# A selective-scan block with a planned order of issue: longer planned TensorE times, and state columns copied after the C product

## The chip, the cores and the metric

The kernel runs on one core of one Trainium2 chip. The metric is the device time of one execution in microseconds (us); the time before is the median of three runs, 4419.52 us (4413.35 to 4423.57). A further execution was taken with the hardware profiler; all rows of the profile come from that one.

Engines are named as in the profile: PE is TensorE (matmuls; PEld is its weight load), DVE is VectorE, ACT is ScalarE, POOL is GpSimd, SP is SyncE, which issues all transfers here.

## The reference

One layer: a normalised Mamba block with a residual, then a normalised linear layer whose weights are dequantised, with a residual. 4096 positions, model width 1024, inner width 2048, 16 states per channel. Cut to what matters:

```python
proj = layernorm(x) @ in_proj_w                    # 1024 -> 2 * 2048
x, z = split(proj); xc = silu(causal_conv4(x))
ssm_p = einsum('bdl,ed->ble', xc, x_proj_w)         # 64 + 16 + 16 rows
dt_r, Bm, Cm = rmsnorm of its three parts
dt = softplus(einsum('blr,dr->bdl', dt_r, dt_proj_w) + dt_bias)
def step(h, inp):                                   # over the positions
    h = exp(dt_t[..., None] * A) * h + dt_t[..., None] * B_t[:, None, :] * x_t[..., None]
    y = einsum('bdn,bn->bd', h, C_t)
    return (h, y)
y = (ys + D_param * xc) * silu(z)
x = hidden + einsum('bdl,hd->blh', y, out_proj_w)
x = x + layernorm(x) @ dequantised(W).T + bias
```

## The kernel before, in words

Channels lie on the 128 partitions, positions along the free axis. Positions are taken in chunks of 512 (`TC`) for the matmuls and in blocks of 256 (`TS`) for the scan. The scan is cut into units: a chunk, a block `s`, a group `g` of four channel tiles, a half `hf` of it (two channel tiles), and a pair `k` of states. That makes 1024 units, each with a scan of two channel tiles, two states and 256 positions. A unit has three steps:

- `unit_b`: POOL multiplies `u` (dt times x) by B into `h`, a tile of 128x1024 (L972), and ACT puts the carried first columns into it (L974, four columns). Three units ahead.
- `unit_e`: ACT makes four exponentials, 128x256 each, into two PSUM tiles `da` (L984), one for each state. One unit ahead.
- `unit_s`: DVE scans, one `tensor_tensor_scan` of 128x512 for each state (L997). Then ACT copies the last column of each scan to `state` (L1001), from which the next block's first columns are made, and the scan is multiplied by C. PE then transposes the product 128x128 at a time and adds it up in `py` (L1014, eight matmuls a unit); at the end of a half, ACT copies `py` out, and an epilogue transposes it back and multiplies by `silu(z)`.

`unit_s` has two forms. With `on_pool` the scan writes to `h`, and POOL multiplies all of `h` by C in one instruction (L1005). Otherwise the scan writes over `da` in PSUM, and DVE multiplies it into `h`, one instruction of 128x512 for each state (L1003). Which form a unit takes is decided while the program is recorded, by comparing the summed planned times of POOL and of DVE (`order.load`).

Buffers: seven `h` tiles (`hp`), four `da` tiles in four PSUM banks (`ps_a`), one `py` (`ps_y`). Accesses to a PSUM bank by different engines are kept in order, readers too; that is how a copy out of `da` and a product out of `da` come to wait for each other in the order in which they are recorded.

Around the units run the large matmuls as background: input projection (`ips`, `zps`), output projection (`ops`) and the last layer (`fps`). Each is three passes on split fp32 values, 128x512 wide (L610, L611, L612). `pull` records as much of them between units as keeps pace with the units.

The order in which every engine issues its instructions is not the recorded one. The class `Order` records all instructions with their accesses (`read`), gives each a planned time (`cost`: the time until the engine can take the next, and the time until the result is there), and plays the whole program through (`schedule`). At each step the engine that can start earliest issues the ready instruction that was recorded first; buffers, transfers and the delay until another engine sees a result (`SEE`) are part of that play. `tie` then fixes the resulting order on every engine. On the chip each engine takes its instructions in that fixed order, and waits where one's inputs are late.

For PE, `cost` has three cases: matmuls into `xps`, wide float32r matmuls by their number of columns `n`, and the rest, which are fp32 transposes.

Of the kernel before, what the change touches and what calls it, by code (L numbers as in the profile page):

```python
# [20 lines left out]
ALU = mybir.AluOpType  # L21
# [6 lines left out]
TS = 256  # L28
# [19 lines left out]
class Order:  # L48
# [112 lines left out]
    def cost(self, r, e, n, silu):  # L161

        op = r.opcode
        if e == 0:
            name = str(r.outs[0])
            if "xps" in name:
                g = 223
            elif "float32r" in str(r.ins[0].dtype):
                g = 6 + 0.434 * n
            else:  # L170
                g = 0.85 * n
            return g, g + 164
        if e == 1:
            if op == "LoadActFuncSet":
                return 1300, 1300
            if op == "TensorCopy":
                d = 170 + 0.815 * n
            else:
                wide = sum(getattr(x, "bass_ap", None) is not None for x in r.ins) > 1
                d = 200 + 1.02 * n if wide else 195 + 0.84 * n  # L180
            if n < 32:
                return 95, 190
            if silu:
                d += 1400
            elif str(r.outs[0].bass_ap.space).endswith("PSUM"):
                return d - 56, d + 17
            return d - 100, d
        if e == 2:
            d = 180 + 2.15 * n
            if op == "TensorTensor" and "pow" in str(r.op):  # L190
                d = 400 + 157 * n
            return d - 40, d
        if e == 3:
            d = 140 + 1.05 * n
            if op == "BNStats":
                d = 676
            elif op == "TensorScalarPtr" and r.is_tensor_tensor_scan:
                d = 150 + 2.085 * n
            elif op == "TensorScalarPtr" and r.is_scalar_tensor_tensor:
                d = 230 + n  # L200
            return d - 82, d
        return 430, 0
# [126 lines left out]
def mamba_ffn_kernel(ctx, tc, hs, in_w, conv_w, conv_b, xp_w, dt_w, dt_b, a_log, d_par, out_w,  # L329
                     dt_ln, b_ln, c_ln, q_scales, q_vals, f_bias, out):  # L330
    nc = tc.nc
# [11 lines left out]
    sizes = [TC] * (L // TC)  # L343
# [4 lines left out]
    NCH = len(sizes)  # L348
# [637 lines left out]
    def unit_s(v, py):  # L986

        c, s, g, hf, k = v["at"]
        cc = bts[c, s, k][1]
        h, da = v.pop("h"), v.pop("da")  # L990
        cb_ = cc.unsqueeze(2).to_broadcast([P, 2, 2, TS])
        g0 = g * 4 + 2 * hf
        on_pool = order.load[2] + POOL_MORE < order.load[3]
        for n in range(2):
            flat = da[n].rearrange("p a b -> p (a b)")
            hflat = h[:, n].rearrange("p a b -> p (a b)")
            nc.vector.tensor_tensor_scan(hflat if on_pool else flat, flat, hflat, 0.0, ALU.mult, ALU.add)  # L997
        for n in range(2):
            last = (h[:, n] if on_pool else da[n])[:, :, TS - 1]
            if not (c == NCH - 1 and s == sizes[c] // TS - 1):  # L1000
                nc.scalar.copy(state[:, g0:g0 + 2, 2 * k + n], last)  # L1001
            if not on_pool:
                nc.vector.tensor_tensor(h[:, n], da[n], cb_[:, n], ALU.mult)  # L1003
        if on_pool:
            nc.gpsimd.tensor_tensor(h, h, cb_, ALU.mult)  # L1005
        hc = h
        terms = [(n, hc[:, n]) for n in range(2)]
        if k == 0:
            terms.insert(0, (-1, v["pre"][3][hf]))
        for n, src in terms:  # L1010
            for tb in range(NTS):
                for j in range(2):
                    i = tb * 2 + j
                    nc.tensor.matmul(py[:, i * P:(i + 1) * P], src[:, j, tb * P:(tb + 1) * P], ident, is_transpose=True,  # L1014
                                     start=(n < 0 and i == 0), stop=(k == N // 2 - 1 and n == 1), skip_group_check=True)
# [44 lines left out]
    state = cst.tile([P, ND, N], F32, name="state")  # L1060
# [104 lines left out]
    for i, v in enumerate(units):  # L1165
        c, s, g, hf, k = v["at"]
        if k == 0:
            py = ps_y.tile([P, TC], F32, tag="py", name="py")
        ahead(i + B_AHEAD, unit_b)
        ahead(i + E_AHEAD, unit_e)  # L1170
        unit_s(v, py)
        v.clear()
        if k == EPI_N and pend is not None:
            pull(until=("z", pend[0], pend[2], 2))
            with tc.high_priority(1000):
                epilogue(*pend)
            pend = None
        pull(total * min(1.0, (i + LEAD) / len(units)))
        b = blocks.index((c, s, g)) + 1
        if b < len(blocks):  # L1180
            if hf == 0 and k == PREP_N:
                if blocks[b][1:] == (0, 0):
                    pull(until=("x", c + 1))
                with tc.high_priority(1000):
                    pres[blocks[b]] = prep_group(*blocks[b])
            if g == NG - 1 and hf == 1:
                c2, s2, _ = blocks[b]
                bts[c2, s2, k] = load_bc(c2, s2, k)
        if k == N // 2 - 1:
            with tc.high_priority(1000):  # L1190
                yt = tmp.tile([P, NTS, 2, P], F32, tag="tmp", name="yt")
                nc.scalar.copy(yt.rearrange("p a b c -> p (a b c)"), py)
            pend = (c, s, g, hf, yt)
# [35 lines left out]
```

## Time and profile before

| What | Value |
|---|---|
| Median of three runs | 4419.52 us (4413.35 to 4423.57) |
| Profiled execution, its own time | 4422.55 us |
| Its span, first to last instruction | 4420.8 us |
| Mean granted TensorE clock | 0.968 |
| B product on POOL, L972, 1024 times | 2423.9 us, 2388 ns each |
| Exponentials on ACT, L984, 4096 times | 1858.6 us, 473 ns each |
| Scans on DVE, L997, 2048 times | 1378.4 us into `da`, 1044.9 us into `h` |
| C product on POOL, L1005, 441 times | 1055.4 us, 2396 ns each |
| Transposes into `py`, L1014, 8192 out of `h` | 1116.6 us, 280 ns each |

Busy time is the union of an engine's instructions, so a PE row's time can overlap its neighbours: PE's instructions are pipelined, and 280 ns for one does not mean one every 280 ns; the distance between starts tells that. A row of the waits says which engine's which line stood idle, and what ended the idle time. Idle time of an engine costs something only where that engine's next work is needed.

### The profile page before, as it was taken

To read this page: it belongs to the slowest core of one execution; us is meant where nothing else is said; L and a number is where in the kernel's file an instruction comes from. 1 tells how busy PE (TensorE), PEld (TensorE's weight loads), DVE (VectorE), ACT (ScalarE), POOL (GpSimd) and SP (SyncE) were. 2 spreads that over 40 slices of the span, in tenths; PEclk is the share of its full clock that TensorE was granted. 3 is DMA by queue.
4 is the path that set the end of the run, shared out by engine and by line. 5 is a ranking of instruction groups with operands and counts; after the bars stand their busy time and mean duration, and the time that the engine had idled before them with its cause. 6 is when DMAs were issued, how large, how long until landed. Compare 5 with 4: busy or idle time off the path is not lost.

```text
span 4420.8 us, 73712 instructions
## 1 busy us (share of the span) xinstructions
PE 4072.3 (92%) x23658; PEld 3451.4 (78%) x23658; DVE 3908.0 (88%) x4842; ACT 3573.4 (81%) x9854; POOL 3853.4 (87%) x2234
## 2 busy tenths in 40 slices
PE   8988899999988999999999999999999999998887
PEld 6767778777876887788777888788877878887776
DVE  5588889998999989999899999999989999998882
ACT  5788888888887888888888789888888877877671
POOL 0678799899997999999999999999998999999791
PEclk9989999999999999999999999999999999999987
DMA  8868866567678765987568875788566898988765
GB/s 261 270 226 286 289 215 217 178 201 222 187 249 273 238 216 174 298 263 246 180 209 272 254 255 184 250 277 277 189 200 215 302 320 264 308 256 275 241 223 189
DMA packets 693843, 1066.39 MB, mean 241 GB/s; under 512 B 63816, under 2 KB 488832, under 8 KB 692432
## 3 DMA queue, kind: packets, MB, share of 16 engines
q1 hardware_dynamic: 693456, 1061.68, 74.1%
q8 instruction: 187, 3.06, 0.3%
q14 instruction: 200, 1.64, 0.1%
HBM read 815.85 MB, written 245.63 MB: 240 GB/s over the span
## 4 chain that ended last, share of the span: by engine, by line
PE 47%; ACT 13%; POOL 13%; DVE 10%; DMA 8%; issue 4%; SPq 1%; DVEq 0%; POOLq 0%; ACTq 0%
PE py L1014 11%; POOL h L972 7%; ACT da L984 4%; DVE da L997 4%; POOL h L1005 4%; PE ops L610 3%; PE ops L611 3%; PE ops L612 3%; PE ips L610 3%; PE ips L612 3%; PE ips L611 3%; PE zps L610 2%; PE zps L611 2%; PE zps L612 2%; DVE h L1003 2%
## 5 line engine op out<-in xcount | busy, mean ns | idle before, releaser
L972 POOL TENSOR_TENSOR h<-xl,bb 128x1020 f32<-128x1020 f32 x1024 | 2423.9, 2388 | 214.7 <-PE py L1014 201.5
L984 ACT ACTIVATE da<-dt,amat 128x256 f32<-128x256 f32 x4096 | 1858.6, 473 | 186.0 <-DVE h L1003 143.4
L997 DVE TENSOR_TENSOR_SCAN da<-da,h 128x512 f32<-128x512 f32 x1166 | 1378.4, 1213 | 66.0 <-POOL h L972 26.5
L1014 PE MATMUL py<-ident,h 128*128 128x128 f32 x8192 | 1116.6, 280 | 97.9 <-POOL h L1005 73.7
L1014 PEld LDWEIGHTS py<-ident,h 128*128 128x128 f32 x8192 | 972.2, 144 | 219.2 <-POOL h L1005 103.1
L1005 POOL TENSOR_TENSOR h<-h,cc 128x1024 f32<-128x1024 f32 x441 | 1055.4, 2396 | 80.8 <-ACT state L1001 71.6
L997 DVE TENSOR_TENSOR_SCAN h<-da,h 128x512 f32<-128x512 f32 x882 | 1044.9, 1208 | 44.4 <-ACT da L984 32.5
L1003 DVE TENSOR_TENSOR h<-da,cc 128x512 f32<-128x512 f32 x1166 | 755.4, 677 | 49.0 <-ACT state L1001 48.0
L610 PE MATMUL ops<-yh,wt 128*128 128x512 f32 (+1 forms) x1152 | 457.2, 398 | 19.5 <-DMA yh<-y 5.8
L611 PE MATMUL ops<-yh,wt 128*128 128x512 f32 (+1 forms) x1152 | 431.4, 375 | 2.4 <-DMA yh<-y 2.2
L612 PE MATMUL ops<-yh,wt 128*128 128x512 f32 (+1 forms) x1152 | 431.0, 374 | 0.0
L610 PE MATMUL zps<-nh,wt 128*128 128x512 f32 x896 | 365.9, 408 | 6.9 <-DVE nh L409 2.8
L612 PE MATMUL zps<-nh,wt 128*128 128x512 f32 x896 | 358.4, 400 | 0.0
L611 PE MATMUL zps<-nh,wt 128*128 128x512 f32 x896 | 357.9, 399 | 0.0
L610 PE MATMUL ips<-nh,wt 128*128 128x512 f32 x768 | 316.1, 412 | 20.2 <-DVE ssm L721 8.4
L688 DVE SCALAR_TENSOR_TENSOR pre<-ips,cw,pre 128x511 f32<-128x511 f32 (+2 forms) x384 | 281.3, 733 | 48.6 <-ACT pre L685 41.6
L612 PE MATMUL ips<-nh,wt 128*128 128x512 f32 x768 | 307.2, 400 | 0.0
L611 PE MATMUL ips<-nh,wt 128*128 128x512 f32 x768 | 306.7, 399 | 0.0
L1001 ACT COPY state<-da 128x2 f32<-128x2 f32 x1098 | 158.8, 160 | 150.0 <-DVE da L997 144.5
L610 PEld LDWEIGHTS ops<-yh,wt 128*128 128x128 f32 x1152 | 223.0, 194 | 53.0 <-DVE xb L835 7.7
L612 PEld LDWEIGHTS ops<-yh,wt 128*128 128x128 f32 x1152 | 222.0, 193 | 36.4
L611 PEld LDWEIGHTS ops<-yh,wt 128*128 128x128 f32 x1152 | 223.6, 194 | 30.8 <-DMA yh<-y 4.7
(163 smaller groups left out, 7159.3 us busy)
## 6 DMA issues: line engine op xcount, KB each, us to landing
wt<-wi SPq DMA_DIRECT2D x416, 512.0 KB, 4.3
wt<-wo SPq DMA_DIRECT2D x288, 512.0 KB, 5.3
wt<-wf SPq DMA_DIRECT2D x144, 512.0 KB, 4.8
yh<-y SPq DMA_DIRECT2D x224, 256.0 KB, 6.2
xl<-xc SPq DMA_DIRECT2D x64, 512.0 KB, 6.3
bb<-b SPq DMA_DIRECT2D x128, 256.0 KB, 5.8
cc<-b SPq DMA_DIRECT2D x128, 256.0 KB, 6.4
ze<-sz SPq DMA_DIRECT2D x128, 256.0 KB, 4.2
```

Source lines behind the costliest of these rows:

```text
L610: nc.tensor.matmul(ps, wk[:, 0, k % 4, :], hi, start=(k == 0), stop=False)
L611: nc.tensor.matmul(ps, wk[:, 0, k % 4, :], lo, start=False, stop=False)
L612: nc.tensor.matmul(ps, wk[:, 1, k % 4, :], hi, start=False, stop=(k == KT - 1))
L688: nc.vector.scalar_tensor_tensor(o, ps[:, 0:sz - 3 + k], cw[:, m, k:k + 1], o, ALU.mult, ALU.add)
L972: nc.gpsimd.tensor_tensor(h[:, :, :, 1:], u[:, js, 1:].unsqueeze(1).to_broadcast([P, 2, 2, TS - 1]), bb[:, :, 1:].unsqueeze(2).to_broadcas ...
L984: nc.scalar.activation(da[n][:, j, :], dt[:, 2 * hf + j, :], AF.Exp, scale=amat[:, d, 2 * k + n:2 * k + n + 1])
L997: nc.vector.tensor_tensor_scan(hflat if on_pool else flat, flat, hflat, 0.0, ALU.mult, ALU.add)
L1001: nc.scalar.copy(state[:, g0:g0 + 2, 2 * k + n], last)
L1003: nc.vector.tensor_tensor(h[:, n], da[n], cb_[:, n], ALU.mult)
L1005: nc.gpsimd.tensor_tensor(h, h, cb_, ALU.mult)
L1014: nc.tensor.matmul(py[:, i * P:(i + 1) * P], src[:, j, tb * P:(tb + 1) * P], ident, is_transpose=True, start=(n < 0 and i == 0), stop=(k = ...
```

## The change

Two things are edited. In `Order.cost` the planned PE times are raised: `xps` from 223 to 234 ns, wide matmuls from 6 + 0.434 n to 10 + 0.45 n, transposes from 0.85 n to 0.9 n (n columns). These numbers are used by the planner alone; no instruction is different for them, but the order of issue is.

In `unit_s` the state copies are recorded elsewhere. On POOL units the two copies of two columns become one of four columns (both states), behind both scans and ahead of the product, which overwrites `h`. On DVE units the copy of a state is recorded behind that state's product, instead of ahead of it. The last block of all still makes no copy.

```diff
             if "xps" in name:
-                g = 223
+                g = 234
             elif "float32r" in str(r.ins[0].dtype):
-                g = 6 + 0.434 * n
+                g = 10 + 0.45 * n
             else:
-                g = 0.85 * n
+                g = 0.9 * n
             return g, g + 164
...
-        for n in range(2):
-            last = (h[:, n] if on_pool else da[n])[:, :, TS - 1]
-            if not (c == NCH - 1 and s == sizes[c] // TS - 1):
-                nc.scalar.copy(state[:, g0:g0 + 2, 2 * k + n], last)
-            if not on_pool:
+        keep = not (c == NCH - 1 and s == sizes[c] // TS - 1)
+        st = state[:, g0:g0 + 2, 2 * k:2 * k + 2]
+        if on_pool:
+            if keep:
+                nc.scalar.copy(st.rearrange("p j n -> p n j"), h[:, :, :, TS - 1])
+            nc.gpsimd.tensor_tensor(h, h, cb_, ALU.mult)
+        else:
+            for n in range(2):
                 nc.vector.tensor_tensor(h[:, n], da[n], cb_[:, n], ALU.mult)
-        if on_pool:
-            nc.gpsimd.tensor_tensor(h, h, cb_, ALU.mult)
+                if keep:
+                    nc.scalar.copy(st[:, :, n], da[n][:, :, TS - 1])
```

## The prediction

> **What bounds the kernel now.** I read the page's busy shares first, then the stretches, the waits, the groups and the timeline.
>
> ```profile
> span 4420.8 us, 73712 instructions
> PE 4072.3 (92%) x23658; PEld 3451.4 (78%) x23658; DVE 3908.0 (88%) x4842; ACT 3573.4 (81%) x9854; POOL 3853.4 (87%) x2234
> ...
> PE 47%; ACT 13%; POOL 13%; DVE 10%; DMA 8%; issue 4%; SPq 1%; DVEq 0%; POOLq 0%; ACTq 0%
> ```
>
> The second line is busy time by engine, the last the chain of waits that ended last. No engine bounds the whole: the chain passes from PE to ACT, POOL and DVE and back.
>
> ```profile
> 1658.00:2210.00 552.00, 525.46 (x3045) 444.15 (x3044) 518.01 (x632) 468.90 (x1333) 519.92 (x298) 0.98 0.73 232
> 2210.00:2763.00 553.00, 528.64 (x3096) 446.13 (x3096) 526.09 (x644) 478.37 (x1355) 530.45 (x303) 0.99 0.73 235
> 2763.00:3315.00 552.00, 528.67 (x3062) 444.54 (x3061) 518.89 (x636) 477.42 (x1343) 525.73 (x301) 0.99 0.74 239
> ```
>
> In the middle of the run (length of the stretch, then busy PE, PEld, DVE, ACT, POOL, then granted clock) PE, DVE and POOL are each busy for 94 to 96%: three engines nearly full, and ACT at 85 to 87%. What is left to win is their waits for each other:
>
> ```profile
> POOL h L972 <- PE py L1014: 201.5, 133, 12.5
> ACT state L1001 <- DVE da L997: 144.5, 197, 3.2
> ACT da L984 <- DVE h L1003: 143.4, 251, 3.7
> PEld py L1014 <- POOL h L1005: 103.1, 98, 5.2
> ...
> POOL h L1005 <- ACT state L1001: 71.6, 51, 5.9
> ...
> DVE h L1003 <- ACT state L1001: 48.0, 51, 4.1
> ...
> DVE h L997 <- ACT da L984: 32.5, 25, 3.5
> ...
> PEld py L1014 <- DVE h L1003: 28.5, 51, 3.5
> ```
>
> Columns: waiter, waited for, us in total, times, longest. The second, fifth and sixth lines are the state copy (L1001): it waits for scans, and both C products (L1005 on GpSimd, L1003 on VectorE) wait for it.
>
> **The change: the copies.** Counts from both orders of issue: ACT goes from 9856 to 9445 instructions; 822 copies out of `h` become 411, the 1098 out of `da` stay. PE, DVE, POOL and SP keep their counts (SP 3133, so no transfer is added), and the same 441 units run their product on GpSimd.
>
> ```profile
> L1003 DVE TENSOR_TENSOR h<-da,cc 128x512 f32<-128x512 f32 x1166 | 755.4, 677 | 49.0 <-ACT state L1001 48.0
> L974 ACT COPY h<-cy 128x4 f32<-128x4 f32 x1024 | 192.9, 197 | 55.9 <-PE py L1014 52.7 <-POOL cy L893 0.3
> L1001 ACT COPY state<-da 128x2 f32<-128x2 f32 x1098 | 158.8, 160 | 150.0 <-DVE da L997 144.5
> L1001 ACT COPY state<-h 128x2 f32<-128x2 f32 x822 | 146.1, 188 | 32.3 <-DVE h L997 29.6
> ```
>
> *Two in one (GpSimd units).* A four-column copy is not in the trace under this name; L974 writes four columns in 197 ns. So ACT sheds 411 × (2 × 188 − 197) ns = 74 us of busy time. ACT has 4420.8 − 3573.4 = 847 us idle, so most is worth nothing. In the chain of waits, summed by line, L1001 holds 19.7 us; 411 of 1920 copies go, 21%, hence 4 us. POOL's 71.6 us stay: the merged copy waits for the second scan, as the second copy did. Ends: −24 us (a third of the 71.6, if ACT was late because of the first copy) to +4 us (9 ns more, 411 times, ahead of POOL). I take −4.
>
> *Behind the product (VectorE units).* Only on-chip order changes: scan, copy, product becomes scan, product, copy. DVE's 48.0 us (51 waits) for ACT go; queued behind such a wait are the next scans and evictions on DVE. How much reaches the end? DVE has 10% of the chain and idles 5 to 6% in the middle; between none and all of 48.0 I take 14, a little under a third, for three engines share the bound. The price is at `da`: its buffer came free after the product, now only after the copy, so the next exponential (L984) starts a copy later, at most 251 × 0.160 = 40 us of ACT time. It hurts where a scan then waits for the exponential: 25 such waits by `h` scans and 14 by `da` scans (16.8 us in the same view), 39 × 0.16 = 6 us. Net −8; ends −48 and +40. The Trainium skill, "PSUM — Partial Sum Buffer", section "PSUM bank collisions raise a hardware error", demands an order between any two engines that touch one bank, two readers included. That speaks against the edit: copy and product never overlap, only their order turns. By the rule alone the wait would merely move and the sum of this part be 0; the trace has the unequal side, 48.0 us on the nearly full DVE against time on ACT.
>
> **The change: the order of issue.** No instruction is added here. The planner's TensorE times are longer: 6 + 0.434 × 512 = 228.2 ns becomes 10 + 0.45 × 512 = 240.4, a transpose 108.8 becomes 115.2. What does the chip take?
>
> ```profile
> 2006.98 0.39 PE L610 MATMUL zps<-nh,wt 128*128 128x512 f32 x1
> ...
> 2007.21 0.39 PE L611 MATMUL zps<-nh,wt 128*128 128x512 f32 x1
> ...
> 2007.43 0.39 PE L612 MATMUL zps<-nh,wt 128*128 128x512 f32 x1
> ...
> 2007.66 0.39 PE L610 MATMUL zps<-nh,wt 128*128 128x512 f32 x1
> ```
>
> First column: start. Starts stand 0.22 to 0.23 us apart (median over all wide matmuls 230 ns; transposes 109). So the old plan fits the undisturbed rate, and the new one is 5% too slow. The Trainium skill, "TensorE: Matmul & The Clock Gate", section "Back-to-back issue gap", gives N/2.4 + 2.5 ns warm, 215.7 ns for 512 columns. By that figure the new plan would be 11% too slow, and the loss per unit worked out below would be some 0.3 us instead of 0.175; the trace's 230 ns decides.
>
> A plan too slow on PE lets PE arrive early: per unit 9.9 wide matmuls (10176/1024) × 12.2 ns + 8.5 transposes × 6.4 ns = 0.175 us. Where did things move? I weighted each engine's instructions, in both orders, with the old trace's median durations (PE with its median intervals), and averaged over units, in us of that engine's own work: scan transposes L1014 stand 1.75, 1.45, 1.55 earlier and 0.29 later by quarters of the run (mean −1.1); products on POOL −1.3 on average, products on DVE −1.15; the B products L972 +0.3. The background matmuls behind the last scan are the same, 51.6 us, so the tail is not touched.
>
> Two readings follow. First, `h` buffers (seven) are returned 1.1 us earlier and claimed 0.3 us later: 1.4 us more room against the greatest wait, POOL for L1014, 201.5 us in 133 waits, 1.5 us each. In the last 553 us, where the quarter shows no such room, lie 35.4 us of it; of the other 166 I take half away, 83 us, and pass on POOL's share of the chain, 13%: −11 us. Ends: 0 and −83. Second, PE's own waits for products: transposes moved no further than the products they read (−1.1 against −1.3 and −1.15), so I cost this at nothing. Its cover is that common shift. If it fails, each of the 98 + 51 weight-load waits grows by 0.175 us, 26 us; the far end is 0.175 us in each of 1024 units, 179 us.
>
> **Sum.** −4 − 8 − 11 = −23 us. The trace's execution took 4422.55 us (span 4420.8 and 1.75 around it), so it would be 4399.5; the runs' median, 4419.52, lies 3 us lower: 4397.
>
> **Rivals.** *Slower: PE comes early and stands.* Place: L1014's weight loads behind L1005 and L1003. Price: if a fifth of the units (205) pay 0.175 us each and the copies bring nothing, +36, 4455 us. It decides once PE's load waits for products (103.1 + 28.5 = 131.6 us) grow by more than the 23 us won elsewhere. For: PE has 47% of the chain and the new plan is further from the trace. Against: products moved up as far as their readers.
> *Larger gain.* POOL's wait falls by 83 us and half counts instead of 13%, DVE's 48.0 by half too: −42 − 24 = −66, 4354 us. For: POOL at 96% in the middle. Against: that PE is as full.
> *Nothing to see.* DVE's wait turns into ACT's and POOL is held by PE anyway: 4420. About 0.2% (9 us) is what a measurement can tell from no change. For: the engines' work, 74 us of ACT aside, is unchanged.
> *The plan does not move anything* is excluded by the shifts above.
>
> **How the numbers follow.** Forecast (−23, its own range 4375 to 4410) 0.43; larger gain 0.11; nothing 0.14; slower 0.32: a reshuffle of the whole order on three nearly full engines can lose as easily as win, and only the copies have a known sign. Hence faster 0.54, same 0.14, slower 0.32. The range takes in the slower case to +36 and the larger gain to −75: 4345 to 4456; I leave about 6% below and 12% above.
>
> **What would show it.** Right: no wait of the product on DVE for ACT; ACT busy near 3500 us; POOL's wait for L1014 near 120 us; PE's load waits for products near 132 us; exponentials waiting on the copy's path no more than 40 us longer. Wrong: PE's load waits above 155 us, POOL's wait unchanged, or more scans waiting for L984 than 39.

## The result and the profile after

The changed kernel takes 4439.1 us (median of six runs, 4431.4 to 4444.5) where the kernel before took 4421.9 beside it: a ratio of 1.004, 95% interval 1.0027 to 1.0054, so 17 us slower. The prediction said 23 us faster. The profiled execution is the fastest of the changed kernel's six, with a span of 4429.6 us.

The first lines of the page after, span and busy time by engine:

```profile
span 4429.6 us, 73586 instructions
PE 4088.3 (92%) x23658; PEld 3425.2 (77%) x23658; DVE 3903.2 (88%) x4842; ACT 3525.0 (80%) x9443; POOL 3853.7 (87%) x2234
```

ACT is 48 us less busy; the copies out of `h` alone fill 67 us less (146.1 before, 79.3 now). Every other engine has the same number of instructions as before; PE's busy time is 16 us longer all the same. The time went mostly into waits. The same three stretches in the middle as before the change (length, busy PE, PEld, DVE, ACT, POOL, then granted clock):

```profile
1658.00:2210.00 552.00, 524.19 (x3020) 437.82 (x3019) 512.60 (x626) 458.10 (x1252) 517.90 (x296) 0.99 0.71 231
2210.00:2763.00 553.00, 527.15 (x3058) 438.78 (x3058) 516.10 (x632) 465.25 (x1271) 521.35 (x299) 1.00 0.72 233
2763.00:3315.00 552.00, 528.96 (x3050) 440.15 (x3049) 517.77 (x636) 469.15 (x1276) 524.94 (x301) 0.99 0.73 237
```

In the second stretch, where the difference is greatest, DVE fell from 526.09 to 516.10 us and POOL from 530.45 to 521.35: the engines that carry the scan get through less in the same time, while the granted clock is not lower. The waits after (waiter, waited for, us in total, times, longest):

```profile
ACT state L1008 <- DVE h L1006: 246.1, 241, 3.5
POOL h L972 <- PE py L1017: 187.4, 126, 14.2
PEld py L1017 <- POOL h L1003: 101.2, 126, 5.8
...
ACT da L984 <- DVE h L997: 93.8, 121, 2.4
POOL h L1003 <- ACT state L1002: 89.9, 71, 5.4
...
PEld yps L422 <- ACT yhi L421: 66.8, 87, 3.4
...
DVE h L997 <- ACT da L984: 47.1, 25, 5.2
...
DVE da L997 <- ACT da L984: 42.3, 28, 4.6
...
PEld dps L924 <- ACT da L984: 28.2, 42, 1.9
...
PEld py L1017 <- DVE h L1006: 20.2, 40, 4.0
```

Lines behind the edit have new numbers: L1014 is now L1017, the product on DVE L1006, on POOL L1003, the copies L1008 and L1002. Three things are to be seen. The product on DVE waits for ACT no more (48.0 us before, no row now), but scans wait for exponentials, 47.1 + 42.3 = 89.4 us where it was 49.3: what the product gained, the next scans paid. PE waits for ACT in the epilogue (`yps`) and in the dt stage (`dps`) far longer than it did. These are the rows of before for those two places, and between them that of scans into PSUM:

```profile
PEld yps L422 <- ACT yhi L421: 23.9, 37, 1.8
...
DVE da L997 <- ACT da L984: 16.8, 14, 4.6
...
PEld dps L924 <- ACT da L984: 4.5, 12, 1.4
```

And PE's load waits for products, the place named by the rival that had it slower, fell: 101.2 + 20.2 = 121.4 against 131.6. The copies themselves take what was forecast (line, engine, operation, shapes, count | busy us, ns of one | idle before):

```profile
L1006 DVE TENSOR_TENSOR h<-da,cc 128x512 f32<-128x512 f32 x1166 | 751.4, 679 | 0.4
...
L1008 ACT COPY state<-da 128x2 f32<-128x2 f32 x1098 | 162.9, 160 | 248.9 <-DVE h L1006 246.1
...
L1002 ACT COPY state<-h 128x4 f32<-128x4 f32 x411 | 79.3, 193 | 20.5 <-DVE h L997 17.8 <-POOL h L972 0.7
```

In the timeline of the changed kernel (start, us, instruction) one such copy holds up ACT:

```profile
2305.76 1.27 DVE L1006 TENSOR_TENSOR h<-da,cc 128x512 f32<-128x512 f32 x2
...
2306.47 0.16 ACT L1008 COPY state<-da 128x2 f32<-128x2 f32 x1 [0.61 <-DVE h L1006]
```

ACT stood 0.61 us until the first product was through. In this kernel's order the next exponential into that buffer comes after the copy.

One more reading shows where the time is lost. The start of the scan of every unit stands in the trace; unit 448 of 1024 began at 2071.0 us before and at 2056.3 after, the last unit at 4319.3 and 4331.2. The changed kernel wins 15 us in the first part and loses 27 us from there to the last unit. The tail behind it is 101.5 and 98.4 us. The same two parts are given for the orders below.

### The profile page after: what moved, and what is told of

Its sections match the earlier page's. It is cut to its first block, busy times and chain, and to the rows that moved or that the text cites. A ratio compares the mean times of both kernels' runs of the same rounds, so it can differ in the third digit from the quotient of the medians.

```text
span 4429.6 us, 73586 instructions
## 1 busy us (share of the span) xinstructions
PE 4088.3 (92%) x23658; PEld 3425.2 (77%) x23658; DVE 3903.2 (88%) x4842; ACT 3525.0 (80%) x9443; POOL 3853.7 (87%) x2234
## 5 line engine op out<-in xcount | busy, mean ns | idle before, releaser
L972 POOL TENSOR_TENSOR h<-xl,bb 128x1020 f32<-128x1020 f32 x1024 | 2424.7, 2389 | 210.9 <-PE py L1017 187.4
L984 ACT ACTIVATE da<-dt,amat 128x256 f32<-128x256 f32 x4096 | 1841.8, 474 | 146.1 <-DVE h L997 93.8
L997 DVE TENSOR_TENSOR_SCAN da<-da,h 128x512 f32<-128x512 f32 x1166 | 1380.2, 1216 | 83.0 <-ACT da L984 42.3
L1017 PE MATMUL py<-ident,h 128*128 128x128 f32 x8192 | 1105.8, 279 | 80.7 <-POOL h L1003 56.4
L1003 POOL TENSOR_TENSOR h<-h,cc 128x1024 f32<-128x1024 f32 x441 | 1055.4, 2397 | 104.2 <-ACT state L1002 89.9
L1017 PEld LDWEIGHTS py<-ident,h 128*128 128x128 f32 x8192 | 961.0, 143 | 208.3 <-POOL h L1003 101.2
L997 DVE TENSOR_TENSOR_SCAN h<-da,h 128x512 f32<-128x512 f32 x882 | 1040.6, 1210 | 70.0 <-ACT da L984 47.1
L1006 DVE TENSOR_TENSOR h<-da,cc 128x512 f32<-128x512 f32 x1166 | 751.4, 679 | 0.4
L1008 ACT COPY state<-da 128x2 f32<-128x2 f32 x1098 | 162.9, 160 | 248.9 <-DVE h L1006 246.1
L610 PEld LDWEIGHTS ops<-yh,wt 128*128 128x128 f32 x1152 | 223.7, 195 | 50.0 <-DMA wt<-wo 6.6
L974 ACT COPY h<-cy 128x4 f32<-128x4 f32 x1024 | 191.4, 195 | 75.8 <-PE py L1017 68.3
L612 PEld LDWEIGHTS ops<-yh,wt 128*128 128x128 f32 x1152 | 222.5, 193 | 36.1
```

The source lines that it names most:

```text
L610: nc.tensor.matmul(ps, wk[:, 0, k % 4, :], hi, start=(k == 0), stop=False)
L612: nc.tensor.matmul(ps, wk[:, 1, k % 4, :], hi, start=False, stop=(k == KT - 1))
L972: nc.gpsimd.tensor_tensor(h[:, :, :, 1:], u[:, js, 1:].unsqueeze(1).to_broadcast([P, 2, 2, TS - 1]), bb[:, :, 1:].unsqueeze(2).to_broadcas ...
L974: nc.scalar.copy(h[:, :, :, 0], cy[:, js, 2 * k:2 * k + 2].rearrange("p j n -> p n j"))
L984: nc.scalar.activation(da[n][:, j, :], dt[:, 2 * hf + j, :], AF.Exp, scale=amat[:, d, 2 * k + n:2 * k + n + 1])
L1008: nc.scalar.copy(st[:, :, n], da[n][:, :, TS - 1])
```

## The experiments

Ratios are to runs of the kernel before on the same chip, with 95% intervals.

### The change taken apart

**Both copy edits, old planned times.** The `unit_s` part of the change alone.

> Both copy edits, with the old planned TensorE times. Theory A (a copy that waits for the product on DVE blocks ACT's queue, and what stands behind it comes late): slower than before by 10 to 20 us, nearly the whole of the change's +17, with ACT's wait for the product near 250 us and DVE's wait before scans near 150 us, as in the changed kernel. Theory B (the longer planned TensorE times make a worse order): same as before or up to 15 us faster. Theory C (any new order scatters by some 10 to 20 us, whatever it was made of): any sign.

Measured: 4432.2 us, 1.0018 (1.0009 to 1.0027).

**The longer planned times alone.**

```diff
-                g = 223
+                g = 234
...
-                g = 6 + 0.434 * n
+                g = 10 + 0.45 * n
...
-                g = 0.85 * n
+                g = 0.9 * n
```

> Only the longer planned TensorE times; copies as before. Theory A: same as before within 9 us. Theory B: slower by 12 us or more. Theory C: any sign, and the sum of this one and of the copies alone is not the +17 us of both together.

Measured: 4429.1 us, 1.0006 (0.9997 to 1.0016).

**Two copies in one on GpSimd units alone.**

```diff
+        if on_pool:
+            if keep:
+                nc.scalar.copy(st.rearrange("p j n -> p n j"), h[:, :, :, TS - 1])
...
+            for n in range(2):
+                if keep:
+                    nc.scalar.copy(st[:, :, n], da[n][:, :, TS - 1])
+                nc.vector.tensor_tensor(h[:, n], da[n], cb_[:, n], ALU.mult)
```

> Only the two copies in one on GpSimd units; old planned times. Theory A: same or up to 8 us faster, since nothing waits for more than before. Theory C: any sign up to 20 us.

Measured: 4424.6 us, 0.9994 (0.9984 to 1.0003).

**The copy behind the product on VectorE units alone.**

```diff
+            for n in range(2):
+                nc.vector.tensor_tensor(h[:, n], da[n], cb_[:, n], ALU.mult)
+                if keep:
+                    nc.scalar.copy(st[:, :, n], da[n][:, :, TS - 1])
```

> Only the copy behind the product on VectorE units; old planned times. Theory A: slower by 10 to 20 us, ACT's wait for the product on DVE near 250 us, the product's wait for ACT gone. Theory B: same as before or faster by up to 15 us. Theory C: any sign.

Measured: 4438.3 us, 1.0027 (1.0016 to 1.0038). In this kernel L1007 is the product and L1009 the copy; its waits:

```profile
ACT state L1009 <- DVE h L1007: 197.9, 194, 3.7
...
DVE da L997 <- ACT da L984: 59.3, 47, 4.0
```

The wait between product and copy turned round, as theory A said, and scans into PSUM wait 59.3 us for exponentials where 16.8 was seen before. For 399 VectorE units (those among units 192 to 895) I measured the way round one PSUM buffer, means in us:

| | before | copy behind |
|---|---|---|
| end of first scan to start of its product | 2.37 | 1.50 |
| end of that product to start of its copy | −1.83 | 0.80 |
| end of that product to first exponential of the unit two later | 0.40 | 1.45 |
| end of second product to end of that unit's last exponential | 1.84 | 3.23 |
| end of last exponential to that unit's scan | 1.12 | 0.78 |

Before, the copy lay mostly beside the second scan, off this way. Behind the product it lies between product and exponential. The product comes 0.87 us sooner after the scan and the exponential 1.05 us later after the product. The two nearly cancel: from the end of the first scan to the start of the product and from its end to the exponential it was 2.37 + 0.40 = 2.77 us, now 1.50 + 1.45 = 2.95, 0.18 us more. What the scan has left in hand behind its last exponential shrank from 1.12 to 0.78 us.

Theory A fitted this kernel. It fitted both copy edits together less well: 8 us where 10 to 20 were expected, and ACT's wait for the product was 177.9 us where 250 were. The next two kernels put it to the test.

### How far does a new order scatter?

**The kernel before with 1 ns more on planned wide matmuls.**

```diff
-                g = 6 + 0.434 * n
+                g = 7 + 0.434 * n
```

> The kernel before with 1 ns more on the planned wide matmuls and nothing else: a control for how far the time scatters when the order is made anew. Theory A (the copy behind the product is the cause, by delaying the exponentials): within 6 us of before. Theory C (any new order scatters by 10 to 20 us): as likely 10 us off as not.

Measured: 4421.8 us, 0.9986 (0.9974 to 0.9998).

**The copy behind the product, with the same 1 ns.** Edit as in the last two diffs.

> The copy behind the product, with the same 1 ns: a second order for the same edit. Theory A: slower than before by 6 to 18 us again, first exponential about 1.4 us behind the product and scans into PSUM waiting some 60 us for exponentials. Theory C: no better than a coin whether it is slower than before, and the 12 us do not come back.

Measured: 4414.3 us, 0.9974 (0.9961 to 0.9987). The same edit that was 12 us slower is 11 us faster with 1 ns in the plan. The way round the buffer is as in the other one (first exponential 1.42 us behind the product), and so are the waits:

```profile
ACT state L1009 <- DVE h L1007: 184.6, 198, 3.2
...
DVE da L997 <- ACT da L984: 53.0, 43, 4.8
```

So the moved wait is real in both, and it does not decide the time: theory A failed here. A single order tells little at this size. Each part of the change but the merge was therefore run in several; the other kernels, the next two among them, have one each.

**The kernel before without its copies out of `da`.** Leaves out the carried state of the VectorE units.

```diff
-            if not (c == NCH - 1 and s == sizes[c] // TS - 1):
+            if on_pool and not (c == NCH - 1 and s == sizes[c] // TS - 1):
```

> Leaves out the 1098 copies out of da, so the carried state of those columns is not kept and the output is not the reference's; all else as before. It says what the copies cost where they stand. Theory A: the copies of before lie beside scans and products, so it is only 0 to 10 us faster than before, and 12 to 22 us faster than with the copies behind. If the copies themselves were the cost on either side of the product, it is 15 us or more faster than before.

Measured: 4381.6 us, 0.9903 (0.9886 to 0.992). Without the copies it is 44 us faster, beyond what theory A allowed and more than the 24 us between the two orders of one edit.

**The longer times for the first 45% of the program only.**

```diff
+            self.early = i < 0.45 * len(self.rec)
...
+                g = 10 + 0.45 * n if self.early else 6 + 0.434 * n
```

> The longer planned TensorE times for the first 45% of the recorded program, the old ones for the rest; copies as before. With the longer times alone unit 448 began 27 us earlier than before and the end was no earlier. If the plan's choice of times works stage by stage, the 27 us stay: 4400 us, 20 to 30 us faster. If the lead is spent again whatever the plan behind it (the later stages are held by something that the earlier ones run ahead of), it ends within 6 us of before.

Measured: 4414.2 us, 0.997 (0.9959 to 0.998). A gain of 13 us, between the two expectations. In its trace unit 448 began 17.5 us earlier than before, the last unit 1.7 us earlier: most of the lead was spent again, though the second part was planned with the old times and the copies ahead.

### More orders of each edit

**The changed kernel with 1 ns more, and 1 ns less, on wide matmuls** (11 + 0.45 n and 9 + 0.45 n).

> The changed kernel with 1 ns more on its planned wide matmuls (11 + 0.45 n). Theory C (the change has next to no price of its own; each new order lands within some 12 us either way): anywhere between 12 us faster and 17 us slower than before. Theory D (both edits together do cost the +17 us): slower by 8 us or more.

> The changed kernel with 1 ns less on its planned wide matmuls (9 + 0.45 n). Theory C: anywhere between 12 us faster and 17 us slower than before, and not tied to the run with 1 ns more. Theory D: slower by 8 us or more.

Measured: 4457.5 us, 1.007 (1.0058 to 1.0082), and 4439.1 us, 1.0035 (1.0022 to 1.0047). The first lies beyond theory C, the second fits both: theory D is the likelier.

**Both copy edits, old times, 1 ns more and 1 ns less** (7 + 0.434 n and 5 + 0.434 n).

> Both copy edits, old planned times with 1 ns more on wide matmuls. Theory C: with the copies edits at 0 ns (+8 us) and this one and the next, a mean within 6 us of before. A price of the copy edits: slower by 5 us or more, as at 0 ns.

> Both copy edits, old planned times with 1 ns less on wide matmuls. Theory C: between 12 us faster and 12 us slower than before. A price of the copy edits: slower by 5 us or more.

Measured: 4417.0 us, 0.9978 (0.9969 to 0.9988), and 4426.9 us, 1.0004 (0.9994 to 1.0014). The mean with the first order (1.0018) is no change: no price of the copies shows under the old times.

**The longer times alone, 1 ns more and 1 ns less** (11 + 0.45 n and 9 + 0.45 n).

> The longer planned TensorE times alone, copies as before, with 1 ns more on wide matmuls (11 + 0.45 n). If the longer times have a price of their own of some 15 us: slower than before by 8 us or more. If the price comes only with the copy behind the product: within 10 us of before, either way.

> The longer planned TensorE times alone, copies as before, with 1 ns less on wide matmuls (9 + 0.45 n). A price of their own: slower by 8 us or more. A price only together: within 10 us of before, either way.

Measured: 4441.9 us, 1.0043 (1.0029 to 1.0056), and 4427.6 us, 1.0006 (0.9995 to 1.0016). One answers to each of the two readings; by themselves they settle nothing.

**The longer times with the copy behind the product, without the merge.**

> The longer planned times and the copy behind the product, but two copies on GpSimd units as before. A price only together: slower by 10 us or more. If the merged copy is what goes with the longer times: within 8 us of before.

Measured: 4432.4 us, 1.0016 (1.0008 to 1.0025), 7 us slower. By its number it falls to the second reading, that the merge goes with the longer times; its interval, 4 to 11 us, reaches past 10, and the scatter is larger than the 2 us between the readings, so the merge's part stays open.

All orders in one table. Ratios are from the runs; the two parts (to the start of unit 448, and from there to the start of the last unit) come from each one's profiled execution.

| planned times, copy | orders | ratios | mean | part one, us | part two, us |
|---|---|---|---|---|---|
| old, ahead (before, +1 ns, merge alone) | 3 | 1, 0.9986, 0.9994 | 0.9993 | 2071.0, 2061.6, 2072.5 | 2248.3, 2251.5, 2252.8 |
| old, behind (with the merge or without) | 5 | 1.0018, 1.0027, 0.9974, 0.9978, 1.0004 | 1.0000 | 2050.5 to 2072.9 | 2261.1 to 2267.4 |
| longer, ahead | 3 | 1.0006, 1.0043, 1.0006 | 1.0018 | 2043.4, 2054.0, 2053.8 | 2275.4, 2285.2, 2265.6 |
| longer, behind (the change and its kin) | 4 | 1.004, 1.007, 1.0035, 1.0016 | 1.0040 | 2048.4 to 2062.0 | 2274.9 to 2293.0 |

By means, at 4425 us: the copy behind costs 3 us alone and 10 us under the longer times; the longer times cost 11 us with the copy ahead and 18 us with it behind; both together 21 us. The spread within a row is 6 to 24 us, so the first of these numbers is not told from nothing, and the second and third are not firm by themselves: two of the three orders with the longer times alone are only 3 us slower. Firmer is what pools more orders: the mean is 0.9998 over the eight with the old times and 1.0031 over the seven with the longer ones, 15 us more, though the two sets overlap; and all four orders like the changed kernel are slower than all three of the first row. Part two is 2248 to 2253 us in the first row and longer in every other order. That is not simply the price of an edit there: the 45% kernel, which has neither edit in its second part, takes 2264.1 us for it, behind a first part of 2053.5. Part of a lead won early is spent later, so only the whole time tells what an edit costs.

### What the longer times do, and the copies' wait

In a kernel with the longer times alone (11 + 0.45 n) these waits stand:

```profile
ACT state L1001 <- DVE da L997: 189.3, 265, 4.6
...
PEld yps L422 <- ACT yhi L421: 66.3, 90, 2.5
...
ACT h L974 <- PE py L1014: 35.3, 57, 4.7
...
PEld dps L924 <- ACT da L984: 24.9, 50, 1.0
```

PE's wait for `yhi` is 66.3 us, as in the changed kernel (66.8), and 23.9 before. Summed over all rows of each trace, ACT's waits for PE are 212 to 230 us in the three orders with the longer times alone (290 to 332 in the three of the first row), its waits for DVE 436 to 443 (363 to 373), PE's load waits for ACT 227 to 244 (175 to 194), and DVE's for POOL 60 to 79 (37 to 50). With the copy behind the product the longer times move the first three sums the same way (ACT's waits for PE 332 to 371 us in the five orders with the old times, 261 to 302 in the four with the longer ones; its waits for DVE 350 to 375 and 408 to 440; PE's load waits for ACT 190 to 207 and 238 to 259).

A planner that takes PE to be slow puts what needs a PE result later into ACT's order, behind more work for the scan. That can be counted, since a trace has ACT's instructions in the order of issue. For each instruction of a kind, take the number of exponentials that ACT issued ahead of it, and compare with the kernel before; the table has the mean difference in exponentials.

| kernel | `yhi` L421 (epilogue) | `r` out of `dps` (dt stage) | `pre` L785 (out of `zps`) | copies out of `da` |
|---|---|---|---|---|
| before, 1 ns more | 0.18 | 0.10 | −0.03 | 0.00 |
| longer times alone, three orders | 1.9 to 2.3 | 3.3 to 3.7 | 4.3 to 5.4 | 0.0 to 0.1 |
| the changed kernel | 2.26 | 3.52 | 5.46 | 0.65 |
| old times, copy behind, five orders | −0.6 to −0.2 | −0.5 to 0.5 | 0.5 to 1.4 | 0.6 |
| shorter times (below) | −1.60 | −2.30 | −2.99 | 0.04 |

The first three kinds read what PE has written. Under the longer times they stand two to five exponentials later, at 473 ns each 1 to 2.5 us of ACT's work, in every order. With the copies ahead ACT then waits less for PE and more for DVE, and PE, which is done early against its plan, waits for ACT. That this later place is what costs the time is the likely reading; no run takes it away alone.

**Shorter planned times** (212; 2 + 0.418 n; 0.8 n).

> Planned TensorE times 5% shorter than before (212; 2 + 0.418 n; 0.8 n), copies as before. If a plan is best where its times are those of the chip: slower than before, by 5 to 20 us. If the cost simply grows with the planned time: faster by 5 to 15 us, with less of TensorE's waits for ACT (175.5 us of weight loads before, 227 to 244 with the longer times).

Measured: 4504.8 us, 1.0178 (1.0164 to 1.0192), 78 us slower. Its waits on ACT:

```profile
ACT h L974 <- PE py L1014: 87.1, 125, 2.5
```

On ACT's side it is the mirror image: what reads PE's results stands earlier in its order (last row of the table), and it waits for PE for 458 us in all, against 294 before. PE's load waits for ACT did not mirror: 222 us, again more than the 175.5 of before. Of the three sets of times tried the old ones are best, and the error cost far more when PE was planned too fast, in the one order that was run.

**Copies of the same number that wait for nothing.** On VectorE units they read `dt` in SBUF instead of `da`; the carried state is not the scan's.

```diff
-                nc.scalar.copy(state[:, g0:g0 + 2, 2 * k + n], last)
+                nc.scalar.copy(state[:, g0:g0 + 2, 2 * k + n], last if on_pool else v["pre"][0][:, 2 * hf:2 * hf + 2, TS - 1])
```

> The copies of VectorE units take their two columns from dt in SBUF, ready long before, instead of from da, so the carried state is not the scan's and the output is not the reference's; their number and order of recording stay. If what the copies cost is ACT's time for 1098 instructions: within 12 us of before. If it is the wait for the scan and the order in the bank: 30 us or more faster, like the kernel that leaves them out (-44 us).

Measured: 4388.4 us, 0.9917 (0.9905 to 0.993), 37 us faster.

```profile
L1001 ACT COPY state<-dt 128x2 f32<-128x2 f32 x1098 | 127.2, 193 | 5.4 <-POOL cy L892 5.2
```

The copies last 193 ns each, longer than out of `da`; neighbours overlap, so that all of them fill 127.2 us of ACT's time where those out of `da` filled 158.8. With that work still there, 37 of the 44 us are gone. So most of what the copies cost is their waiting for the scan and their place in the bank's order, not ACT's time; the two are not told apart. The edit also frees the next block's first columns from waiting for the scan; in the trace of before, the instruction that reads the state (L892) stood idle for a copy 0.3 us in all, so that is not where the 37 us lay on the chip. One order was run.

**The copy on VectorE itself**, behind the scan, so that neither engine waits for the other over it.

```diff
-                nc.scalar.copy(state[:, g0:g0 + 2, 2 * k + n], last)
+                (nc.scalar.copy if on_pool else nc.vector.tensor_copy)(state[:, g0:g0 + 2, 2 * k + n], last)
```

> On VectorE units VectorE itself copies the last columns, right behind the scan; old planned times. The wait between two engines is gone, as in the kernels without it (-37 and -44 us), but VectorE gets 1098 small instructions, at some 0.1 us each 110 us on an engine busy for 95% in the middle. If the instructions weigh more: slower by 20 to 60 us. If the wait does: faster by 10 to 30 us.

Measured: 4413.1 us, 0.997 (0.9958 to 0.9983), 14 us faster.

```profile
L1005 POOL TENSOR_TENSOR h<-h,cc 128x1024 f32<-128x1024 f32 x459 | 1098.9, 2397 | 62.1 <-ACT state L1001 50.7 <-issue 5.7 <-DVE h L997 1.2
...
L1001 DVE COPY state<-da 128x2 f32<-128x2 f32 x1062 | 158.4, 149 | 0.3
```

Each lasts 149 ns on VectorE, with next to no idle time before it (0.3 us in all), and the kernel still gains. But the edit did a second thing: VectorE's planned load now holds the copies, so 18 more units were given to GpSimd (459 instead of 441, hence 1062 copies and not 1098), and 36 products of 678 ns, some 24 us, left VectorE. How much of the gain is the copy's place and how much this shift was not tried. The kernel beats both others, as do the longer times up to 45% (4414.2 us) and the copies behind with 1 ns more (4414.3 us; 4417.0 with the merge); its lead is of the size of the scatter, and only one order of it was run.

## Why the prediction was wrong, point by point

**Two in one, −4 us.** Right as far as can be told: −2 us, interval −7 to +1. The merged copy takes 193 ns where 197 was taken. POOL's wait for it rose to 89.9 us instead of keeping 71.6; in the kernel with the merge alone it is 78.4.

**Copy behind the product, −8 us.** The first half held: DVE's 48.0 us went in every order. The price was mis-sized. It was put at 39 waits × 0.16 us = 6 us: the 39 waits of before, each longer by one copy. The delay was about right, 0.18 us from the scan to the next exponential, but the number of waits was not held: with less left in hand, 65 to 73 scans waited for exponentials in the five orders with the old times, each some 1.2 to 1.5 us, in all 88 to 111 us and not 49.3 + 6 (in the changed kernel 53 waits, 89.4 us; the prediction named more than 39 as a sign of being wrong). The 48 us of waits won and the 39 to 61 lost nearly cancel: 3 us slower by the means, not told from nothing. This is what the prediction held against itself from the Trainium skill, "PSUM — Partial Sum Buffer", section "PSUM bank collisions raise a hardware error": two readers of a bank on different engines need an order. The prediction inferred that turning it would merely move the wait. The runs side with that reading, a sum of 0, rather than with the −8 of the text; −8 is within the scatter.

**The order of issue, −11 us and nothing for PE.** This is the step that failed: the gain of 11 us, and the term for PE's own waits that was put at nothing. By the means the longer times cost 11 us by themselves and 18 with the copies behind, 15 over all orders. The prediction took the mean shift of transposes, products and B products in the orders for a gain in `h` buffers, and let half of POOL's wait go. POOL's wait for L1014 went from 201.5 to 187.4 us, not to 120, and to 186 to 193 with the longer times alone. What the text did not weigh are the instructions that moved the other way: the ACT work that reads PE's results, which in the changed kernel stands 2 to 5 exponentials later than before. The mean shifts of transposes and products say nothing about it, and PE's new waits are there: its weight loads waited 250 us for ACT, 175.5 before (epilogue 23.9 to 66.8, dt stage 4.5 to 28.2).

**The cover for PE, transposes moved as far as their products.** It held: PE's load waits for products fell from 131.6 to 121.4 us.

**The slower rival, +36 us, 0.32.** Its sign is right, and PE does come early against its plan and stand. Its place is wrong: the added waits are not at the transposes for products but for ACT. Its size is twice the 17 us measured, so its price was not confirmed either.

**The tail is untouched.** Right: 101.5 us before, 98.4 after, behind the start of the last unit.

**The size of plan scatter.** The text allowed for a reshuffle that can lose as easily as win, and set no number beside it. Two orders that differ by 1 ns in the plan are up to 24 us apart with the same edits, as large as the whole effect forecast.

**The planned times against the trace.** The prediction had the new plan 5% too slow by the row of 230 ns, worked out 0.175 us a unit from it, and then put the price at nothing. The Trainium skill, "TensorE: Matmul & The Clock Gate", section "Back-to-back issue gap", gives 215.7 ns for a wide matmul by its formula, which it calls the gap of an isolated one. The kernel with shorter times plans 216.0, with `xps` and the transposes shortened as well, and is 78 us slower. Here the row of the trace was the one to plan by.

What stays open: that ACT's later place is what costs the time is read from its order and from waits that moved the same way in every order with longer times; no run took just that shift away. Whether the copy behind the product has a price of its own under the longer times (10 us by the means, within the scatter) is not settled. Why part one gains from the longer times and the lead is spent again was not tried beyond the 45% kernel.

## What to carry to other kernels

When a planner fixes the order of issue, its times are inputs to be fitted to the trace: here 5% longer cost 0.2 to 0.4% by the means of several orders, 5% shorter 1.8% in one. Before one order is compared with another, make a few orders of the same code with a change that should not matter, and see how far the time scatters; an effect smaller than that needs several orders of each side. A small copy between two engines is priced by the waits on both sides of it and not by its 160 ns; here turning its order round mostly chose who waits.

## What the runs showed of the hardware

A copy of two columns out of PSUM lasts 149 ns on VectorE and 160 ns on ScalarE; out of SBUF it lasts 188 to 193 ns on ScalarE. Neighbours overlap: 1098 copies of 193 ns filled 127.2 us. Taken out of the order between engines, 1098 such copies were worth 37 us in the one order run, some 34 ns each. Adding 1062 of them to VectorE, and taking 36 products of 678 ns from it, raised its busy time by 42 us (3908.0 to 3949.6), and the kernel became faster.
